# Choosing the experts of an image for six and two blocks of tokens in place of four, two and two

## The chip, the cores and the metric

The kernel runs on one core of one Trainium2 chip. Five engines work side by side, each through its own queue of instructions in order: TensorE (PE in the profile, with its weight loads as PEld), VectorE (DVE), ScalarE (ACT), GpSimd (POOL) and SyncE (SP), which issues most DMAs. The metric is the time of one execution on the device in microseconds (us); a reported time is the median of the runs.

## The reference

The input x is 4 images of 384 channels and 32 by 32 pixels. Layer 0 normalises groups of channels, runs a selective scan over the 1024 pixels in four directions with 16 states per channel, merges the directions, normalises, applies gelu and adds x. Layer 1 takes the pixels as 1024 tokens of 384 values: causal attention with one head is added, and then a mixture of four experts, of which each token uses two. What the change touches is the choice of the two experts:

```python
scores = jnp.einsum('bsd,de->bse', x, gate_w) + gate_b
probs = jax.nn.softmax(scores, axis=-1)
topk_vals, topk_idx = jax.lax.top_k(probs, TOP_K)            # TOP_K = 2 of 4 experts
mask = jnp.sum(jax.nn.one_hot(topk_idx, NUM_EXPERTS, dtype=probs.dtype), axis=-2)
masked = probs * mask
masked = masked / (jnp.sum(masked, axis=-1, keepdims=True) + 1e-09)
h = jax.nn.gelu(jnp.einsum('bsd,edh->ebsh', x, w1) + b1[:, None, None, :], approximate=False)
y = jnp.einsum('ebsh,ehd->ebsd', h, w2) + b2[:, None, None, :]
out = jnp.einsum('bse,ebsd->bsd', masked, y)
```

## The kernel before

**Ticks.** The order of all engines' work is written out by a loop over ticks. There are 768 units of the scan, 192 for each image, and each tick of the first 768 issues one: on ScalarE the decay da (an exponential), on VectorE the product v (front, L697) and the scan h (middle, L703), on GpSimd the product of h of the tick before with the C rows (back, L720), which is ordered behind v of its tick and so runs beside the scan. In image 0 TensorE makes some of the v instead. Every fourth tick TensorE adds four h into y (row, L745).

**Work beside the scan.** Attention and experts of image b are worked out during the scan of image b+1; those of image 3 follow the last tick. They are generators that go_on advances at the end of each tick: those in the list side get a step each tick, those in waiting (attention and experts) a budget of TensorE time. `yield "wait", 1` means: go on next tick; `yield "pe", x` means that about x us of TensorE work were issued, and a side generator stops for the tick when more than 1.0 is used up. What a step issues on VectorE stands in VectorE's queue after the scan of that tick and before v of the next.

**Shared buffers.** slots are eight SBUF buffers of 128 by 1024 floats that everything shares. They are handed out in the order in which they were given back, one tick after that at the earliest. banks are four PSUM banks shared in the same way.

**The choice of experts.** The 1024 tokens of an image are eight blocks of 128. As attention finishes blocks, ready (L1273) is started for a group of blocks: GROUPS = ((0, 4), (4, 2), (6, 2)), as first block and number. For its n blocks it normalises the rows, transposes them, computes the gate scores on TensorE (L1318) and adds the bias (sc, L1328). Then, all on small tensors of VectorE:

- exponents (L1343) and, a tick later, probabilities (L1348): softmax over the four experts;
- choice (L1353): each expert's score is compared with the others in cmp (n x 4 x 4), giving sel, the two best, and cum, running counts per expert;
- two ticks later kept (L1375): mk, the probabilities of the two chosen, normalised again;
- one tick later, with counts over the partitions and over the groups before that TensorE sums into pp: at, the row that a token would take in each expert's list, and from it spot and places, the two rows that it takes (L1427 to L1442). The last group also makes table (L1496): which expert and which rows each of 11 turns of 256 rows works on, and how many rows of the turn are filled (held_rows);
- mk is transposed (pm, L1468) and copied to a slot (mt);
- scatter (L1448): one block per tick, two indirect DMAs of GpSimd write the block's rows to the lists of its two experts in DRAM (xs_d);
- in the tick of the last scatter the shares (L1480 to L1486): for each of the two choices, which expert's row it is, times mk, summed; one tick later mt is stored to gates_d.

When the last group is routed, experts (L1544) loads rows from xs_d and the experts' weights on SP's queue, and works through the turns. For image 3 (alone in the code) the exponents and shares stand elsewhere, and only there are held_rows read, to skip empty rows on TensorE.

## Time and profile before

| | us |
|---|---|
| median of three runs | 3735.69 |
| lowest, highest | 3728.15, 3737.49 |
| the profiled execution | 3733.57 |
| its span, first to last instruction | 3731.8 |
| busy: PE, DVE, ACT, POOL | 3003.4, 2967.0, 2058.5, 1976.4 |
| granted TensorE clock, mean | 0.860 of full speed |

By stages, the busy time of the engines in us (0 to 850 is about image 0's scan, then the scans of images 1 to 3 with the attention and experts of images 0 to 2 beside them, then attention and experts of image 3):

| stretch | PE | DVE | ACT | POOL | DMA share |
|---|---|---|---|---|---|
| 0 to 850 | 555.0 | 736.9 | 614.2 | 526.0 | 0.60 |
| 850 to 1650 | 657.6 | 740.5 | 461.5 | 478.7 | 0.69 |
| 1650 to 2450 | 679.2 | 746.2 | 452.0 | 478.0 | 0.66 |
| 2450 to 3200 | 639.1 | 688.5 | 398.1 | 463.1 | 0.64 |
| 3200 to 3732 | 472.6 | 54.9 | 132.6 | 30.6 | 0.45 |

A row of a stretch is read against its length: VectorE is busy for 746 of 800 us in the third.

The lines of groups on the page give, after the engine and the operation, what is written and read, shapes, count, busy time and mean duration in ns, and the idle time of the engine before them with what ended it. A line that tells one instruction in order of time gives its start and its duration in us.

The choices of experts of images 0, 1 and 2 lie at about 934 to 1013, 1813 to 1897 and 2635 to 2722 us.

### The profile page before, as it was taken

Reading aid. Unit: us, or ns where it says so; the run is one execution under the profiler, and the core shown is the slowest. Engines: PE = TensorE matmul, PEld = TensorE weight load, DVE = VectorE, ACT = ScalarE, POOL = GpSimd, SP = SyncE. Lnnn points to the kernel's source line nnn. Section 1 sums busy time; section 2 is a strip of 40 time slices with the busy share of each in tenths; the row PEclk is TensorE's granted clock in tenths of the full one; section 3 lists DMA queues with packets and bytes.
Section 4 is the critical chain, followed back from the end, with each engine's and each line's share of the span. In section 5 each row is a group of like instructions: output and inputs, shape, how many; then the busy total and the mean of one; then the engine's idle time right before and its main releaser. Section 6 shows DMA issues by size and latency. Waiting matters only on the chain.

```text
span 3731.8 us, 41382 instructions
## 1 busy us (share of the span) xinstructions
PE 3003.4 (80%) x13281; PEld 1796.7 (48%) x13281; DVE 2967.0 (80%) x2338; ACT 2058.5 (55%) x3269; POOL 1976.4 (53%) x931
## 2 busy tenths in 40 slices
PE   4766666778489999769669999769679999788998
PEld 1333333334256555334336656334346665466776
DVE  6899888989979999998999999999989999220000
ACT  5787887556466566355546665445446664342221
POOL 2777667645645555764556656765656666110001
PEclk7677767789689999879779999879689999889997
DMA  5667555444478878644558978563468886215655
GB/s 188 217 255 286 208 209 204 170 166 161 165 242 282 305 269 296 223 172 140 188 200 288 320 250 300 192 211 127 139 226 304 284 291 225 75 62 162 200 188 168
DMA packets 405200, 798.41 MB, mean 214 GB/s; under 512 B 47500, under 2 KB 278620, under 8 KB 404972
## 3 DMA queue, kind: packets, MB, share of 16 engines
q1 hardware_dynamic: 390572, 770.01, 59.5%
q0 software_dynamic: 8192, 25.17, 2.0%
q8 instruction: 118, 1.93, 0.2%
q10 hardware_dynamic: 6208, 0.39, 0.1%
q14 instruction: 110, 0.90, 0.1%
HBM read 680.44 MB, written 115.02 MB: 213 GB/s over the span
## 4 chain that ended last, share of the span: by engine, by line
DVE 44%; PE 33%; ACT 7%; DMA 7%; issue 5%; POOL 2%; SPq 1%; DVEq 0%; ACTq 0%; POOLq 0%
DVE h L703 24%; DVE v L697 14%; PE ph L1680 7%; PE py L1730 6%; PE y L745 3%; DMA du<-dts 2%; DMA w<-in_w 2%; ACT da L196 2%; PE pq L1121 2%; ACT st L196 2%; PE v_end L1730 2%; PE pv L1132 1%; POOL h L720 1%; PE pdt L537 1%; PE y_end L1730 1%
## 5 line engine op out<-in xcount | busy, mean ns | idle before, releaser
L720 POOL TENSOR_TENSOR h<-h,bc 128x1024 f32<-128x1024 f32 x768 | 1812.8, 2364 | 1218.5 <-DVE v L697 1076.4
L703 DVE TENSOR_TENSOR_SCAN h<-da,v 128x1024 f32<-128x1024 f32 x768 | 1749.9, 2283 | 78.7 <-PE v L1009 41.1
L196 ACT ACTIVATE da<-dt,a 128x1024 f32<-128x1024 f32 x768 | 883.2, 1160 | 770.0 <-DVE h L703 643.9
L697 DVE TENSOR_TENSOR v<-du,bc 128x1024 f32<-128x1024 f32 x665 | 858.1, 1290 | 117.6 <-PE y L745 50.4
L745 PE MATMUL y<-h,sel 128*32 128x512 f32 x3072 | 572.1, 708 | 197.4 <-POOL h L720 189.8
L1680 PE MATMUL ph<-turned,w 128*128 128x256 f32 (+1 forms) x2784 | 637.0, 385 | 47.2 <-DMA w<-in_w 42.4
L1680 PEld LDWEIGHTS ph<-turned,w 128*128 128x128 f32 x2784 | 526.2, 194 | 166.8 <-issue 49.9
L1730 PE MATMUL py<-w,ht 128*128 128x384 f32 x1704 | 577.8, 491 | 3.9 <-DMA w<-in_w 3.8
L1730 PEld LDWEIGHTS py<-w,ht 128*128 128x128 f32 x1704 | 319.6, 191 | 259.5 <-issue 38.3
L745 PEld LDWEIGHTS y<-h,sel 128*32 128x32 f32 x3072 | 104.5, 120 | 534.6 <-POOL h L720 308.3
L196 ACT ACTIVATE ht<-ph,b1t 128x256 f32<-128x256 f32 x470 | 197.0, 472 | 281.2 <-PE ph L1680 260.4
L1789 POOL DMA_INDIRECT g<-ysd,places x64 | 83.9, 1310 | 342.8 <-DMA ysd<-yt 327.0
L196 ACT ACTIVATE st<-turn,bt 128x128 f32<-128x128 f32 x832 | 243.5, 546 | 0.1
L1009 PE MATMUL v<-ident,st 128*128 128x128 f32 x824 | 155.0, 350 | 87.1 <-DVE h L703 79.6
L1009 PEld LDWEIGHTS v<-ident,st 128*128 128x128 f32 x824 | 125.8, 182 | 134.4 <-DVE h L703 69.4
L186 ACT ACT_TABLE_LOAD x120 | 154.0, 1283 | 12.3 <-issue 10.2
L537 PE MATMUL pdt<-xd,wdt 12*128 12x512 f32 x184 | 114.8, 753 | 32.4 <-ACT st L196 17.0
L1450 POOL DMA_INDIRECT xsd<-fx,places x32 | 36.5, 1141 | 132.9 <-issue 132.3
L1749 DVE COPY yt<-y_end 128x384 f32<-128x384 f32 x3 | 1.7, 558 | 130.6 <-ACT ht L196 62.9
L1222 PE MATMUL po<-vt,pt 128*128 128x384 f32 x234 | 90.9, 539 | 13.1 <-ACT pt L1112 13.1
L1151 PE MATMUL ss<-axn,qt 128*128 128x512 f32 (+3 forms) x240 | 90.3, 519 | 3.4 <-ACT yb L1232 1.6
L196 ACT ACTIVATE ht<-ht 128x3072 f32<-128x3072 f32 x33 | 91.3, 2766 | 0.4
(411 smaller groups left out, 2710.8 us busy)
## 6 DMA issues: line engine op xcount, KB each, us to landing
w<-in_w SPq DMA_DIRECT2D x528, 384.0 KB
bc<-rows SPq DMA_DIRECT2D x384, 512.0 KB
dt<-dts SPq DMA_DIRECT2D x192, 512.0 KB
du<-dts SPq DMA_DIRECT2D x192, 512.0 KB
dts<-dt SPq DMA_DIRECT2D x48, 512.0 KB
dts<-du SPq DMA_DIRECT2D x48, 512.0 KB
xg<-xsd SPq DMA_DIRECT2D x44, 384.0 KB
ysd<-yt SPq DMA_DIRECT2D x44, 384.0 KB
```

The lines of the kernel that those rows point to most:

```text
L186: nc.scalar.preload_act_table_set(kind)
L196: return nc.scalar.activation(dst, src, f, **more)
L537: nc.tensor.matmul(pss[i], wdt[r, m * P : (m + 1) * P], xd[r, bass.ts(h, 512)], start=True, stop=True,)
L697: return nc.vector.tensor_tensor(u["v"], spread["du4", n], spread["bc", n][:, 0, :], ALU.mult)
L703: nc.vector.tensor_tensor_scan(u["h"][:, ::step], u["da"][:, ::step], u["v"][:, ::step], 0.0, op0=ALU.mult, op1=ALU.add,)
L720: product = units[n]["product"] = nc.gpsimd.tensor_tensor(h, h, spread["bc", n][:, 1, :], ALU.mult)
L745: units[n]["row"] = nc.tensor.matmul(y, sel, h, start=first, stop=last, tile_position=(0, jj * DJ))
L1009: nc.tensor.transpose(u["v"][:, t * P : (t + 1) * P], st[:, t, u["j"] * P : (u["j"] + 1) * P], ident)
L1151: nc.tensor.matmul(ps[:, : e - o], qt[:, c, i * P : (i + 1) * P], xn[o // 512][:, c, : e - o], start=(c == 0), stop=(c == M - 1 and (alone ...
L1222: nc.tensor.matmul(po[:, :C], pts[i][:, j, :], vt[:, j, :], start=False, stop=(j == i))
L1680: nc.tensor.matmul(ps[:, i * BT : i * BT + n], t[:, c, i * P : (i + 1) * P], xt[:, c, :n], start=(c == 0), stop=(c == M - 1),)
L1730: nc.tensor.matmul(pss[i][:, :C], hts[j][:, 2 * c + f, i * P : (i + 1) * P], tiles["2", j, c][0][:, f, :], start=(c == 0 and f == 0), stop ...
```

## The change

For the first three images the normalising, the transposes and the scores stay in groups of four, two and two, but the scores of the first four and the next two go into one tensor sc, and what follows is done once for all six, in a new function chosen: from exponents to shares. The last two blocks stay a group of their own. Image 3 keeps its three groups. Beside this, in all images:

- both choices stand in one tensor two, so that spot comes from one maximum instead of a minimum and a maximum, and the shares from three instructions instead of six;
- cmp is no longer a buffer of its own but a slot (for image 3 a buffer of the scan's decays, which is over by then);
- mk is transposed and copied in parts of up to four blocks, so six blocks take two banks, two slots and two stores to gates_d, the second part one tick after the first;
- held_rows are worked out for image 3 only;
- the small tensors, base and fresh are made large enough for six blocks, and the image's totals move to another column of pp;
- experts waits until all groups of the image are routed.

```diff
-    base = const.tile([P, E, 4], F32, tag="base", name="base")
+    base = const.tile([P, E, 6], F32, tag="base", name="base")
     fresh = {}
-    for n in (2, 4):
+    for n in (2, 4, 6):
...
+        def group_rows(q0, n):
+
+            if q0 + n > 4 and b not in routes:
                 routes[b] = Route(b)
-            return routes[b].rows[:, q0 - 4 : q0 - 4 + n]
+            return [
+                fx0[:, q, :] if q < 4 else routes[b].rows[:, q - 4, :] for q in range(q0, q0 + n)
+            ]
...
+    WIDE = ((0, 6), (6, 2))
...
-        sc = small("sc", name, n, E)
+        groups = GROUPS if alone else WIDE
+        g = [i for i, (g0, gn) in enumerate(groups) if g0 <= q0 < g0 + gn][0]
+        g0, gn = groups[g]
+        if (b, g) not in raw:
+            raw[b, g] = small("sc", f"{b}_{g}", gn, E), []
+        sc, whole = raw[b, g]
         nc.vector.tensor_tensor(
-            sc, pg[:, : n * E].rearrange("p (q e) -> p q e", e=E),
+            sc[:, q0 - g0 : q0 - g0 + n], pg[:, : n * E].rearrange("p (q e) -> p q e", e=E),
             gb.unsqueeze(1).to_broadcast([P, n, E]), ALU.add,
         )
         banks.give(f"pgate_{name}")
-
+        whole.extend(rows)
+        if len(whole) < gn:
+            return
+        yield from chosen(b, g, sc, whole)
...
+    def chosen(b, h, sc, rows):
+
+        alone = b == B - 1
+        name = f"{b}_{h}"
+        groups = GROUPS if alone else WIDE
+        last = len(groups) - 1
+        q0, n = groups[h]
+        parts = [range(o, min(o + 4, n)) for o in range(0, n, 4)]
...
         def choice():
-            cmp = [
-                one.tile([P, 4, E, E], F32, tag=f"cmp{i}", name=f"cmp{i}_{name}")[:, :n]
-                for i in range(2)
-            ]
+            both = cmp_.rearrange("p (i f) -> p i f", i=2)[:, :, : n * E * E]
+            both = both.rearrange("p i (q a b) -> p i q a b", a=E, b=E)
+            cmp = [both[:, i] for i in range(2)]
...
+        if alone:
+            cmp_ = dap.tile([P, L], F32, tag="da", name=f"cmp_{name}")
+        else:
+            cmp_ = yield from slots.take(f"cmp_{name}", P, L)
         cum = choice()
+        if not alone:
+            slots.give(f"cmp_{name}")
...
-        if h == LAST:
-            for i in range(LAST + 1):
+        if h == last:
+            for i in range(last + 1):
                 nc.tensor.matmul(
-                    pp[:, 4 * E : 5 * E], ones, last_of(i, False),
-                    start=(i == 0), stop=(i == LAST),
+                    pp[:, 8 * E : 9 * E], ones, last_of(i, False),
+                    start=(i == 0), stop=(i == last),
...
         spot = small("spot", name, n, 2)
-        two = [small(f"two{i}", name, E, n) for i in range(2)]
+        two = sm.tile([P, 2, E, 6], F32, tag="two", name=f"two_{name}")[:, :, :, :n]
         far = float(2 * E * CAP)
-        nc.vector.scalar_tensor_tensor(two[0], sel, -far, at, ALU.mult, ALU.add)
-        nc.vector.tensor_tensor(two[1], sel, at, ALU.mult)
-        nc.vector.tensor_reduce(
-            spot[:, :, 0], two[0].rearrange("p e q -> p q e"), AX.X, ALU.min
-        )
-        nc.vector.tensor_reduce(
-            spot[:, :, 1], two[1].rearrange("p e q -> p q e"), AX.X, ALU.max
-        )
-        nc.vector.tensor_scalar_add(spot[:, :, 0], spot[:, :, 0], far)
+        nc.vector.scalar_tensor_tensor(two[:, 0], sel, far, at, ALU.mult, ALU.subtract)
+        nc.vector.tensor_tensor(two[:, 1], sel, at, ALU.mult)
+        nc.vector.tensor_reduce(spot, two.rearrange("p i e q -> p q i e"), AX.X, ALU.max)
+        nc.vector.tensor_scalar(spot[:, :, 0], spot[:, :, 0], -1.0, far, ALU.mult, ALU.add)
         nc.vector.tensor_copy(places[b][:, q0 : q0 + n, :], spot)
...
-        pm = yield from banks.take(f"pm_{name}")
-        for q in range(n):
-            nc.tensor.transpose(pm[:E, q * P : (q + 1) * P], mk[:, q, :], ident)
-        yield "pe", 0.12 * n
-        mt = yield from slots.take(f"mt_{name}", E, 512)
-        yield "wait", 1
-        nc.scalar.copy(mt[:, : n * P], pm[:E, : n * P])
-        banks.give(f"pm_{name}")
+        mts = []
+        for part in parts:
+            pm = yield from banks.take(f"pm_{name}_{part[0]}")
+            for q in part:
+                o = (q - part[0]) * P
+                nc.tensor.transpose(pm[:E, o : o + P], mk[:, q, :], ident)
+            yield "pe", 0.12 * len(part)
+            mt = yield from slots.take(f"mt_{name}_{part[0]}", E, 512)
+            mts.append(mt)
+            yield "wait", 1
+            nc.scalar.copy(mt[:, : len(part) * P], pm[:E, : len(part) * P])
+            banks.give(f"pm_{name}_{part[0]}")
...
-        for i in range(2):
-            same = two[i]
-            nc.vector.tensor_tensor(
-                same, at, spot[:, :, i].unsqueeze(1).to_broadcast([P, E, n]), ALU.is_equal
-            )
-            nc.vector.tensor_tensor(same, same, mk.rearrange("p q e -> p e q"), ALU.mult)
-            nc.vector.tensor_reduce(
-                shares[b][:, q0 : q0 + n, i], same.rearrange("p e q -> p q e"), AX.X, ALU.add
-            )
-        yield "wait", 1
-        nc.sync.dma_start(gates_d[b][:, q0 * P : (q0 + n) * P], mt[:, : n * P])
-        slots.give(f"mt_{name}")
+        nc.vector.tensor_tensor(
+            two, at.unsqueeze(1).to_broadcast([P, 2, E, n]),
+            spot.rearrange("p q i -> p i q").unsqueeze(2).to_broadcast([P, 2, E, n]), ALU.is_equal,
+        )
+        nc.vector.tensor_tensor(
+            two, two, mk.rearrange("p q e -> p e q").unsqueeze(1).to_broadcast([P, 2, E, n]),
+            ALU.mult,
+        )
+        nc.vector.tensor_reduce(
+            shares[b][:, q0 : q0 + n, :], two.rearrange("p i e q -> p q i e"), AX.X, ALU.add
+        )
+        yield "wait", 1
+        for part, mt in zip(parts, mts):
+            o = (q0 + part[0]) * P
+            nc.sync.dma_start(gates_d[b][:, o : o + len(part) * P], mt[:, : len(part) * P])
+            slots.give(f"mt_{name}_{part[0]}")
...
         tables[b] = sm.tile([1, 3, NBLK], I32, tag="tables", name=f"tables_{b}")
-        nc.vector.tensor_copy(tables[b], which)
+        kept = 3 if b == B - 1 else 2
+        if kept == 3:
+            held_rows = which[:, 2, :]
...
+            nc.vector.tensor_scalar(held_rows, held_rows, n[:, 0:1], 0.0, ALU.add, ALU.max)
+            nc.vector.tensor_scalar_min(held_rows, held_rows, float(BT))
+        nc.vector.tensor_copy(tables[b][:, :kept], which[:, :kept])
...
-        while (b, LAST) not in routed:
+        groups = GROUPS if alone else WIDE
+        while not all((b, h) in routed for h in range(len(groups))):
```

## The prediction

> **What bounds the kernel now.** I read the page first, then the table by stages, then the order of time of VectorE and of GpSimd around the choice of experts of image 2, then the same stretches of images 0 and 1 and the chain of waits in them.
>
> ```profile
> span 3731.8 us, 41382 instructions
> DVE  6899888989979999998999999999989999220000
> L720 POOL TENSOR_TENSOR h<-h,bc 128x1024 f32<-128x1024 f32 x768 | 1812.8, 2364 | 1218.5 <-DVE v L697 1076.4
> L703 DVE TENSOR_TENSOR_SCAN h<-da,v 128x1024 f32<-128x1024 f32 x768 | 1749.9, 2283 | 78.7 <-PE v L1009 41.1
> L697 DVE TENSOR_TENSOR v<-du,bc 128x1024 f32<-128x1024 f32 x665 | 858.1, 1290 | 117.6 <-PE y L745 50.4
> ```
>
> Until about 3170 us VectorE is full: each of 768 ticks is a product v (1.29 us) and a scan (2.28 us), some 3.58 us, with GpSimd's product of the tick before (2.36 us) beside the scan. Everything else that VectorE does stands between a scan and the next v and lengthens that tick. After 3200 us VectorE is nearly idle and TensorE carries the experts of image 3. So a VectorE instruction saved in images 0 to 2 counts in full where nothing else holds the tick, and one saved in image 3 counts only on its short chain.
>
> The second reading is GpSimd beside it, in the choice of image 2. Columns: start, duration, engine, line.
>
> ```profile
> 2662.00 2.35 POOL L720 TENSOR_TENSOR h<-h,bc 128x1024 f32<-128x1024 f32 x1 [0.56 <-PE place L1405]
> 2664.50 1.80 POOL L1450 DMA_INDIRECT xsd<-fx,places  x1 [0.16 <-issue]
> 2666.61 0.96 POOL L1450 DMA_INDIRECT xsd<-fx,places  x1 [0.30 <-issue]
> 2667.59 2.36 POOL L720 TENSOR_TENSOR h<-h,bc 128x1024 f32<-128x1024 f32 x1
> ...
> 2664.18 1.26 DVE L697 TENSOR_TENSOR v<-du,bc 128x1024 f32<-128x1024 f32 x1
> 2665.47 2.29 DVE L703 TENSOR_TENSOR_SCAN h<-da,v 128x1024 f32<-128x1024 f32 x1
> 2667.67 2.31 DVE L1376 SCALAR_TENSOR_TENSOR mk<-cnt,sc 128x8 f32<-128x8 f32 x1
> 2670.02 0.16 DVE L1377 TENSOR_REDUCE red<-mk 128x2 f32<-128x8 f32 x1
> ```
>
> A pair of scatters (L1450) pushes GpSimd's product back by more than a scan. The tiny mk then takes 2.31 us instead of the some 0.17 of its neighbours: it ends just after the product does (2669.95). So a tick after a pair of scatters is bound by GpSimd, and small work on VectorE under the scatters is partly free. In the pair above no small work preceded v at 2664.18, and the first scatter took 1.80 us, ending after v. The pair at 2659.13 and 2660.46, under the choice of blocks 4 and 5, took 1.03 and 0.97 and delayed nothing.
>
> [...] The trace: a cmp of 32 elements takes 0.19 us, of 64 elements 0.225. From those two I estimate 0.26 for 96.
>
> **The change, part by part.** An instruction that depends on the one before it starts 0.20 to 0.26 us after it, an independent one 0.10.
>
> *What is removed.* Counted in the code: from the exponents to the shares a group has 30 VectorE instructions before and 26 after (the minimum and maximum become one reduction; six share instructions become three). Three groups and a table of 21 made 111 per image; two groups and a table of 13 make 65. So 46 fewer for each of three images, 12 fewer for the last. By their starts in image 2: probabilities and choice 2.11 us for four blocks and 1.92 for two, which become one run of six; seven of its instructions grow by about 0.03, so 2.3. mk and its normalisation: 1.06 and 0.73 plus its blocked first, become 1.1. Places: 0.91 and 0.89 become 0.85. Shares: 1.0 and 0.8 become 0.62. Exponents: 0.34 saved. Table: from 2707.87 to 2709.50, 1.63 saved. The group of blocks 6 and 7: 0.1 at its places, 0.3 at its shares. In all 7.1 us per image.
>
> *What is moved.* Placing and scattering of blocks 0 to 3 now wait for blocks 4 and 5. Call T0 the tick in which the scores of the first four come (v at 2631.86 to v at 2635.83). The scores of 4 and 5 come in T4, those of 6 and 7 in T10. Before, scatters are issued in T5 to T8 (blocks 0 to 3), T9, T10, then T15, T16. After: choice of six in T5, mk in T7, places and first transposes in T8, the second transposes cost one more tick (T9), scatters of blocks 0 to 5 in T10 to T15, blocks 6 and 7 still in T15 and T16. T15 gets four scatters. The choice of 6 and 7 keeps its ticks, so the last scatter and the start of the experts stay in T16. SP's queue: the gates' DMA becomes two in T16, about 0.5 us each of issue with data long ready; xg behind them waits for the scatters anyway.
>
> *The ticks of image 2*, measured before, and after by these rules: v waits for the product; the product waits for the pair and the v before it; a scatter that meets v ends some 0.9 us after it. T0 −0.4; T1 −2.1 (choice of four gone); T3 −1.05 (its mk); T4 −0.85 (its places gone, exponents of six); T5 +0.4 (choice of six instead of two); T7 6.53 to 4.7, −1.8; T8 6.23 to 4.43, −1.8 (no scatters under either now); T10 7.06 to 5.25 (its shares and their blocking gone; eviction stays), −1.8. Then the scatters' new places. T11 0: pair under the scores, choice of 6 and 7 after it. T12 +0.1. T13 4.62 to 6.55, +1.9: pair bare under T12, mk waits. T14 8.01 to 7.1, −0.9: table shorter by 1.63, blocked 0.75. T15 +0.85: shares of six and a short wait. T16 6.59 to 7.65, +1.05: four scatters. T17 +0.2. Sum −6.2. As a check, 7.1 us of instructions less, stalls about the same: about 7.3 us before (T7 2.2, T8 0.9, T10 1.0, T11 0.3, T16 2.2, T17 0.7).
>
> *Other images.* Image 0 has the same order and no idle VectorE there: −6.2. In image 1, VectorE waits 3.94 us for TensorE (y L745) in T0, so T0's gain is lost, and I give back half of T1's: −4.9. Image 3 keeps three groups: its places are 0.1 us shorter in each, its shares 0.4 shorter after the scatter. I take −0.3; none or −0.8 are the ends.
>
> *Unknowns.* cmp now takes one of the eight shared slots and so waits for whoever last read that slot. Slots come back in order of release, and attention's were released several ticks before, so I take 0. The upper end is a transfer of 512 KB still under way, once per image: the longest in the chain of waits is 11.56 us (du<-dts at 2317.34). The reductions over four dimensions are costed as those over three: 0 to 0.1 us each. Could the gain be lost at the experts' start? There VectorE stalls 10.87 us in image 0 and 6.63 in image 2 on a row sum behind the first weights; that chain begins with the last scatter, which itself moves earlier, so I let it through. If it did not pass, half the gain could go.
>
> **Sum.** 6.2 + 4.9 + 6.2 + 0.3 = 17.6 us. The profiled execution took 3733.57: 3716.0. The median of the runs shown is 2.1 above it, so 3718.
>
> **Rivals.** (a) *Absorbed*: TensorE and the weights set the pace at the experts' start, or attention's end holds T1. For it: 18% of the chain is TensorE's outside the last 540 us (33% in all, the tail 14.5%). Against: in T0 to T17 of images 0 and 2 VectorE shows no wait for TensorE. Half the gain, −9: 3727. (b) *Slower: cmp waits for its slot.* Where the slot's last reader is a store of image preparation, VectorE stands between a scan and v, and GpSimd behind it, until that store lands: at 11.56 us in each of three images, 34.7 − 17.6 = +17, 3753. It decides from 5.9 us per image. For it: in image 1 two stores of 512 KB leave at 1829 and 1830, four ticks before the choice of six. Against it: the oldest released slot is taken, and in image 2 no store is near. (d) *Bare scatters.* The small work that covered them is gone. A bare pair makes 5.59 us from product to product (2662.00 to 2667.59), 2.0 more than a tick; seven such and 1 for the four in T15 are 15 per image instead of 7.3: +7.7 − 7.1, nothing gained, 3738. Against it: T10, T11, T13 and T14 do have work of blocks 6 and 7. (c) *More*: each removed instruction gives its full 0.2 us and stalls shrink: 46 × 0.2 × 3, 28 us, 3708. That the change does other than it says I exclude: blocks, places and scatters are all still there.
>
> **How the numbers follow.** Forecast 0.56, (a) 0.17, (b) 0.10, (c) 0.11, (d) 0.06. A measurement of this kernel tells about 0.3%, 11.2 us, from no change. Faster by more: the forecast nearly whole, (c), and a little of (a): 0.68. Within: most of (a), most of (d) and the forecast's edge: 0.21. Slower: (b) and the rest of (d), 0.11. Range 3706 to 3734: from (c) with 2 us of noise to past (a).
>
> **What would show it.** VectorE has 150 instructions fewer (2338 to 2188). T0 to T10 are about 9 us shorter, T11 to T17 about 3 longer. One mk of six blocks per image is short, and the mk of blocks 6 and 7 takes about 2.3 us where it took 0.3. Scatters stand bare in T12 and four of them in one tick. Wrong would be a cmp that waits for a slot, stalls of 14 us or more per image, or experts that start a tick or more later.

## The result and the profile after

The changed kernel takes 3706.61 us (median of 5 runs, 3705.43 to 3712.27) against 3735.69. The ratio is 0.9931, with a 95% interval of 0.9917 to 0.9946: 25.8 us less, between 20.2 and 31.0. The forecast was 17.6 us less, 3718; the median lies 0.6 us inside the lower end of the stated range (3706 to 3734). The profiled execution took 3705.43 us, of which the span is 3703.4.

The lines of the page that answer to those shown of before:

```profile
span 3703.4 us, 41159 instructions
DVE  6898888999979999998999999999999998220000
L720 POOL TENSOR_TENSOR h<-h,bc 128x1024 f32<-128x1024 f32 x768 | 1813.6, 2366 | 1189.3 <-DVE v L697 1033.9
L703 DVE TENSOR_TENSOR_SCAN h<-da,v 128x1024 f32<-128x1024 f32 x768 | 1749.5, 2283 | 78.4 <-PE v L1009 33.4
L697 DVE TENSOR_TENSOR v<-du,bc 128x1024 f32<-128x1024 f32 x665 | 871.2, 1310 | 105.7 <-PE y L745 46.6
```

The scan and the product are what they were; VectorE is as full. Its 2338 instructions are 2188, and GpSimd stands 29 us less idle before its products (1218.5 to 1189.3). Where did this time go from? Every tick has one scan, so the k-th scan of one execution can be set against the k-th of another: a difference that arises between scans 633 and 634 belongs to that tick. T0 is tick 240, 438 and 633 in images 0, 1 and 2. From the starts of the scans in the two traces, after minus before, in us:

| tick | forecast for image 2 | image 2 | image 0 | image 1 |
|---|---|---|---|---|
| T0 | -0.4 | -0.27 | 0.01 | -0.31 |
| T1 | -2.1 | -1.98 | -1.98 | -2.67 |
| T3 | -1.05 | -1.08 | -1.08 | -1.10 |
| T4 | -0.85 | -0.89 | -0.88 | -0.89 |
| T5 | +0.4 | 0.41 | 0.44 | 0.41 |
| T6 | 0 | 0 | -0.71 | 0 |
| T7 | -1.8 | -1.94 | -1.93 | -1.92 |
| T8 | -1.8 | -1.70 | -1.53 | -1.02 |
| T9, T10 | -1.8 | -1.77 | -3.03 | -3.11 |
| T11, T12 | +0.1 | 0.70 | 0.97 | 0.95 |
| T13 | +1.9 | 2.01 | 0.67 | 1.11 |
| T14 | -0.9 | -0.75 | -0.80 | -0.75 |
| T15 to T17 | +2.1 | 2.27 | 2.27 | 2.20 |
| sum | -6.2 | -4.99 | -7.58 | -7.10 |

The same differences, added over longer stretches and for every kernel of this study against the first profile of before. The choices are ticks 240 to 264, 432 to 456 and 632 to 656; the experts are ticks 264 to 360, 456 to 584 and 656 to 767; the rest is all else, with the end of image 3. The ratio is over the timed runs. The runs e5 to e8 were made on another chip and e12 on a third, each beside the kernel before on the same chip, so kernels are compared by their ratios; medians are compared for runs of one chip alone.

| kernel | choices | experts | rest | ratio, 95% interval |
|---|---|---|---|---|
| changed | -20.6 | -11.7 | +4.0 | 0.9931, 0.9917 to 0.9946 |
| e1 changed again | -20.3 | -9.7 | -0.3 | 0.9931, 0.9918 to 0.9944 |
| e2 three groups | -8.2 | -6.2 | +0.3 | 0.9962, 0.9948 to 0.9975 |
| e3 long table | -12.2 | 0.0 | +1.1 | 0.9963, 0.9950 to 0.9976 |
| e4 early scatters | -19.2 | -7.6 | +10.4 | 0.9940, 0.9928 to 0.9953 |
| e5 padded | +4.1 | -8.2 | +0.8 | 0.9999, 0.9990 to 1.0008 |
| e6 before, padded | +9.7 | -3.5 | -1.6 | 1.0031, 1.0019 to 1.0043 |
| e7 lean | -21.6 | -4.1 | -0.7 | 0.9936, 0.9920 to 0.9952 |
| e8 four and four | -31.7 | -1.1 | +11.6 | 0.9935, 0.9919 to 0.9950 |
| e9 early weights | -36.5 | -13.7 | +7.6 | 0.9898, 0.9882 to 0.9914 |
| e10 before, slot | +0.2 | -3.9 | -1.3 | 0.9998, 0.9987 to 1.0008 |
| e11 before again | -0.5 | -3.7 | -1.6 | one run only |
| e12 before, early weights | -17.2 | -4.9 | +10.5 | 0.9959, 0.9947 to 0.9970 |

The first two columns of the changed kernel are the result: 20.6 us in the choices, where 17.3 were forecast, and some 6 to 12 us in the experts' stages between them, where nothing was forecast. The second part is seen in single profiles only: of the timed 25.8 us the choices leave 5.2, and with the interval anything from 0 to 10. The rest lies mostly before the choice of image 0 and behind the last scan. The first of these differs by 4.2 us between the two executions of the kernel before, the second by 5.4 us between the two of the changed kernel, so I read nothing from it.

How a pair of scatters, now bare, pushes the product back is seen in GpSimd's order of time in image 2 of the changed kernel (start, duration, engine, line):

```profile
2658.37 1.01 POOL L1474 DMA_INDIRECT xsd<-fx,places  x1 [0.17 <-issue]
2659.69 1.98 POOL L1474 DMA_INDIRECT xsd<-fx,places  x1 [0.31 <-issue]
2661.69 2.36 POOL L720 TENSOR_TENSOR h<-h,bc 128x1024 f32<-128x1024 f32 x1
2664.21 1.81 POOL L1474 DMA_INDIRECT xsd<-fx,places  x1 [0.17 <-issue]
2666.33 0.96 POOL L1474 DMA_INDIRECT xsd<-fx,places  x1 [0.31 <-issue]
2667.30 2.36 POOL L720 TENSOR_TENSOR h<-h,bc 128x1024 f32<-128x1024 f32 x1
...
2681.61 1.09 POOL L1474 DMA_INDIRECT xsd<-rows,places  x1 [0.15 <-issue]
2683.00 1.06 POOL L1474 DMA_INDIRECT xsd<-rows,places  x1 [0.30 <-issue]
2684.37 0.96 POOL L1474 DMA_INDIRECT xsd<-rows,places  x1 [0.30 <-issue]
2685.63 0.96 POOL L1474 DMA_INDIRECT xsd<-rows,places  x1 [0.30 <-issue]
2686.62 2.35 POOL L720 TENSOR_TENSOR h<-h,bc 128x1024 f32<-128x1024 f32 x1
```

From product to product 5.61 us pass (2661.69 to 2667.30), as the prediction had it for a bare pair (5.59). The four scatters of T15 are there, from 2681.61. VectorE in the same image:

```profile
2630.26 0.18 DVE L1374 TENSOR_TENSOR sc<-sc,red 128x24 f32<-128x24 f32 x1
2630.47 0.26 DVE L1382 TENSOR_TENSOR cmp<-sc 128x96 f32<-128x96 f32 x1
...
2639.24 0.32 DVE L1399 SCALAR_TENSOR_TENSOR mk<-cnt,sc 128x24 f32<-128x24 f32 x1
...
2667.39 2.31 DVE L1399 SCALAR_TENSOR_TENSOR mk<-cnt,sc 128x8 f32<-128x8 f32 x1
```

The comparison starts 0.21 us after the instruction that it depends on: no wait for its slot. The mk of six blocks is short (0.32), and that of blocks 6 and 7, which took 0.29 before, now takes 2.31 beside the product at 2667.30. In images 0 and 1 it takes 1.04 and 1.25.

### The profile page after: what moved, and what is told of

The parts are those of the page before. It is cut to its first block, busy times and chain, and to the rows that moved or that the text cites. A ratio compares the mean times of both kernels' runs of the same rounds, so it can differ in the third digit from the quotient of the medians.

```text
span 3703.4 us, 41159 instructions
## 1 busy us (share of the span) xinstructions
PE 2985.5 (81%) x13251; PEld 1787.3 (48%) x13251; DVE 2948.8 (80%) x2188; ACT 2058.9 (56%) x3266; POOL 1973.0 (53%) x933
## 3 DMA queue, kind: packets, MB, share of 16 engines
q8 instruction: 118, 1.93, 0.2%
## 4 chain that ended last, share of the span: by engine, by line
PE 30%; DVE 29%; DMA 3%; issue 2%; ACT 2%; SPq 1%; POOL 1%; DVEq 0%; POOLq 0%; ACTq 0%
DVE h L703 16%; DVE v L697 10%; PE ph L1714 8%; PE py L1764 7%; PE y L745 2%; DMA w<-in_w 2%; PE v_end L1764 2%; PE y_end L1764 1%; PE pq L1121 1%; PE pv L1132 1%; DMA du<-dts 1%; PE y_end L1714 1%; PE v_end L1714 1%; ACT ht L196 1%; POOL h L720 1%
## 5 line engine op out<-in xcount | busy, mean ns | idle before, releaser
L720 POOL TENSOR_TENSOR h<-h,bc 128x1024 f32<-128x1024 f32 x768 | 1813.6, 2366 | 1189.3 <-DVE v L697 1033.9
L697 DVE TENSOR_TENSOR v<-du,bc 128x1024 f32<-128x1024 f32 x665 | 871.2, 1310 | 105.7 <-PE y L745 46.6
L745 PE MATMUL y<-h,sel 128*32 128x512 f32 x3072 | 564.6, 701 | 208.5 <-POOL h L720 201.5
L186 ACT ACT_TABLE_LOAD x120 | 154.0, 1283 | 12.1 <-issue 10.0
L537 PE MATMUL pdt<-xd,wdt 12*128 12x512 f32 x184 | 112.6, 745 | 36.6 <-ACT st L196 20.3
```

The source lines that it names most:

```text
L186: nc.scalar.preload_act_table_set(kind)
L537: nc.tensor.matmul(pss[i], wdt[r, m * P : (m + 1) * P], xd[r, bass.ts(h, 512)], start=True, stop=True,)
L697: return nc.vector.tensor_tensor(u["v"], spread["du4", n], spread["bc", n][:, 0, :], ALU.mult)
L720: product = units[n]["product"] = nc.gpsimd.tensor_tensor(h, h, spread["bc", n][:, 1, :], ALU.mult)
L745: units[n]["row"] = nc.tensor.matmul(y, sel, h, start=first, stop=last, tile_position=(0, jj * DJ))
```

## The experiments

Each edit is against the changed kernel, or against the kernel before where it says so.

**e1, the changed kernel again**

> The changed kernel, unchanged, a second time. The trace of the changed kernel showed 20.6 us gained in the ticks of the three choices (7.9, 6.8, 5.9) and 11.6 us more between them, in the experts of images 0, 1 and 2 (5.5, 4.6, 1.5), less 3.75 us lost after the last scan. Theory L (the extra belongs to this kernel's order of transfers and ticks): the same three numbers again within 1 us each, time 3705 to 3709 us. Theory R (the extra is how transfers fell in that one execution): the choices again 20 to 21 us, but the experts' 11.6 us differ by 3 us or more, and the time goes with them.

Measured 3705.69 us (3703.52 to 3710.43). The choices repeat to 0.3 us in sum: 7.6, 8.4 and 4.3 against 7.9, 6.8 and 5.9, and every tick from T1 to T17 to 0.02. What differs are a few ticks around them that wait for TensorE (tick 438 by 1.6 us, tick 654 by 1.6). The experts give 5.7, 2.5 and 1.5 in place of 5.5, 4.6 and 1.5; the stretch after the last scan is 1.6 us shorter than before where it was 3.75 longer. So the gain in image 0's experts belongs to the kernel; of image 1's, half moved between two executions; and the loss at the end did not come again. Neither theory holds whole.

**e2, three groups again**

```diff
-    WIDE = ((0, 6), (6, 2))
+    WIDE = GROUPS
```

> Keeps the shorter table and the fused places and shares, and chooses in groups of four, two and two again. Predicted terms: of the 7.1 us of VectorE work per image the table is 1.63 and the fused shares and places about 1.3 (1.0 + 0.8 + 0.8 of shares become about 1.5, places 0.2 less), so merging is about 4.2 per image, 12 us in all. Theory M (merging pays, stalls equal): 8 to 13 us slower than the changed kernel, 3715 to 3720. Rival S (the new scatter places cost more than the merged choice saves): within 4 us of the changed kernel or faster. Where the experts' ticks lie differently, the extra gain of 11.6 us should change by more than 3 us if it comes from the places of the ticks, and stay if it comes from the parts that both share.

3719.24 us, ratio 0.9962: 11.6 us slower than the changed kernel (0.31% of 3735). Its choices give 8.2 us, 12.1 to 12.5 less than with six and two. The merging was forecast at 4.2 per image: theory M. The experts give 6.2, of it 3.4 in image 0, so three groups have a part of that gain too.

**e3, the long table**

```diff
-        kept = 3 if b == B - 1 else 2
+        kept = 3
```

> The changed kernel with the eight instructions of the table's third row worked out for images 0 to 2 too. Theory M (the table stands between scan and product in full): 1.63 us for each of three images, 4.9 us slower, 3711 to 3712. Rival C (a pair of scatters stands over that tick, and the table is covered): less than 1.5 us slower in all.

3718.99 us, 12 to 13 us slower than the changed kernel. The table itself is 1.51, 1.53 and 1.51 us (tick T14 in each image), 4.6 in all, as theory M has it and against C. What the other 7 to 9 us are is not shown. In the trace tick T0 waits 1.2 and 1.3 us longer for TensorE in images 0 and 1 (for attention's output, and for the row sums y), and the experts give 0.0 in place of 10 to 12. But T0 of image 0 comes before anything that this edit adds, and of the experts' loss the largest parts stand in ticks 460 and 530, which move by 2.6 and 1.8 us between the two executions of the changed kernel.

**e4, scatters one tick earlier**

```diff
+        todo = [] if alone else list(range(n))
+        if todo:
+            yield "wait", 1
         mts = []
         for part in parts:
+            if todo:
+                scatter(todo.pop(0))
...
-            for q in range(n):
-                scatter(q)
-                if q < n - 1:
+            while todo:
+                scatter(todo.pop(0))
+                if todo:
                     yield "wait", 1
```

> The changed kernel with the scatters of blocks 0 to 5 begun one tick earlier, beside the transposes of mk, which they don't need. No tick has four scatters then. In the trace of the changed kernel ticks T15, T16, T17 of image 2 are 0.7, 0.3 and 1.3 us longer than before. Theory B (the burst of four costs this): 1.5 to 2.3 us less per image, 5 to 7 us faster than the changed kernel, about 3700. Rival N (a pair costs about 2 us wherever it stands, bare or after another pair): the time stays within 2 us. Should the first pair meet a product v, 0.9 us per image comes back.

3711.93 us, not faster: 5 to 6 us slower by the medians, where rival N had said within 2. In image 2 the burst is gone and T15 to T17 are 2.7 us shorter than in the changed kernel, but T10, T11 and T14, under which the pairs now stand, are 0.8, 1.3 and 0.9 longer: 2.9 given back. In images 0 and 1 the same ticks give back 3.8. This is rival N by the ticks: moving the pairs changes where they cost and gains nothing.

**e5, the changed kernel padded**

```diff
             nc.vector.tensor_tensor(cmp[0], cmp[0], cmp[1], ALU.max)
+            for _ in range(26 if h == 0 and not alone else 0):
+                nc.vector.tensor_tensor(cmp[0], cmp[0], cmp[1], ALU.max)
```

> The changed kernel with 26 VectorE maxima of 96 elements, which change nothing, put into the choice of six of images 0 to 2 (tick T5), 0.25 us each as dependent ones: 6.5 us per image, so the choices last about as long as before the change. The extra gain in the experts of images 0 to 2 was 11.7 and 9.7 us in two executions of the changed kernel, 6.2 with three groups, 7.6 with the early scatters and 0.0 with the long table. Theory A (the experts' gain or loss is how VectorE's ticks fall against TensorE's chain, which any VectorE work in the choice shifts): the experts' gain is another number, differing by 3 us or more from 10, and the total is 19.5 us of padding plus or minus that. Theory O (the gain comes with what the changed kernel emits: stores of the gates later in SP's queue, slots taken for the comparisons): the experts' gain stays at 9 to 12, and the time is 3725 to 3727.

3732.19 us. The padding took more than I had put: in VectorE's order of time

```profile
2647.83 7.57 DVE L1389 TENSOR_TENSOR cmp<-cmp 128x96 f32<-128x96 f32 x26
```

26 in 7.57 us, 0.29 each, and T5 grew by 7.6 us in every image, 22.8 in all. By the ratios the padded kernel is 25.4 us slower than the changed one (19 to 32). The experts give 8.2, with choices that are even longer than before: nearer to theory O, and against A as I had put it, though the time is above O's. No other tick from T1 to T17 moved by more than 0.02 us, so T5 pays for VectorE's work in full.

**e6, the kernel before padded**

```diff
             nc.vector.tensor_tensor(cmp[0], cmp[0], cmp[1], ALU.max)
+            for _ in range(16 if h == 1 and not alone else 0):
+                nc.vector.tensor_tensor(cmp[0], cmp[0], cmp[1], ALU.max)
```

> The kernel before with 16 VectorE maxima of 32 elements, which change nothing, put into the choice of blocks 4 and 5 of images 0 to 2: 0.2 us each, 3.2 us per image. Theory A (where the ticks fall): the experts of images 0 to 2 gain or lose 3 us or more against the kernel before, most likely a gain, since all five kernels tried beside it had none or a gain; total 9.6 us of padding less that, so 3734 to 3744. Theory O (what is emitted): the experts stay within 2 us, and the time is 3743 to 3745.

3744.52 us, at the seam of the two theories: T5 is 3.6 us longer per image, 10.8 in all, and the ratio says 11.6 (7.1 to 16.1). The experts give 3.5 in sum, as much as a second execution of before gives (e11). Inconclusive by the time, but not by the ticks: 342 and 346 are 1.4 and 0.4 us shorter although nothing but padding was added.

**e7, the lean choice**

```diff
             exponents()
             yield "wait", 1
-            probabilities()
...
-            nc.vector.tensor_scalar_add(red, red, 1e-9)
             nc.vector.reciprocal(red, red)
```

> The changed kernel without the normalisation of the probabilities (three VectorE instructions per group) and without the small constant added to the sum of the two kept (one), since the kept two are normalised anyway and their sum is at least the largest exponential, 1. Eight instructions less per image 0 to 2, twelve less in image 3. Theory F (each removed small instruction on the full VectorE gives its 0.2 us): 1.6 us per image in the choices, 4.8 us, and up to 1 us in the last image's chain: 3700 to 3702. Rival H (the instructions of blocks 6 and 7 lie under scatters and give nothing): half of it, 3703 to 3705. The experts' part may shift by some us either way and is read apart.

3707.45 us, ratio 0.9936: no gain. By the ticks, T5 is 0.42 to 0.49 us shorter than in the changed kernel, T7 and T13 0.2 each and T11 0.1, some 1.0 us per image where 1.6 were expected; the three instructions of blocks 6 and 7 in T11 gave 0.12 us instead of 0.6. That is rival H by the ticks. Its 3 us do not show in the time; in this trace the experts gave 4.1 in place of 9.7.

**e8, four and four**

```diff
-    WIDE = ((0, 6), (6, 2))
+    WIDE = ((0, 4), (4, 4))
...
-            cum = sm.tile([P, (24, 8, 8)[h]], F32, tag=f"cum{h}", name=f"cum_{name}")
+            cum = sm.tile([P, (24, 16, 8)[h]], F32, tag=f"cum{h}", name=f"cum_{name}")
```

> The changed kernel with groups of four and four in place of six and two: as few VectorE instructions, the scatters of blocks 0 to 3 in T5 to T8 as before, those of blocks 4 to 7 in T15 to T18. The experts of images 0 to 2 begin two ticks, some 8 us, later. Theory E (TensorE is busy for 96 percent of the experts' stages, so a later start is paid): the experts' stages lose 4 to 8 us per image, time 3715 to 3730. Rival P (VectorE's ticks pay for nothing but their own work there): within 4 us of the changed kernel.

3708.36 us, the same as six and two within the interval: rival P by the time. By the parts neither theory describes it. Of the 31.7 us of the choices 10.8 are tick 262 of image 0, 14.4 us long before: with the experts starting later, no row sum waits behind them there. The experts of images 1 and 2 give back 8.9 and 4.6, as theory E has it, and those of image 0 gain 14.5. Since all this work stands two ticks later, a tick no longer holds the same work in both traces, and of the 11.6 us of the rest 6.3 lie before the first choice.

**e9, the first weights earlier**

```diff
         while not all((b, h) in routed for h in range(len(groups))):
+            if b in tables and fetched[0] < 4 and slots.ready(1 + slots.kept):
+                weights()
             yield "wait", 1
```

> The changed kernel with the first four weight chunks of images 0 to 2 asked for one per tick from the tick of the table on, as far as slots are free, and not all together behind the gathered rows. In the changed kernel VectorE waits 10.6 us at 1046.5 (image 0, third tick before the experts' stage) for the row sums y, which stand in TensorE's queue behind the first expert's ph, and ph waits for weights that were asked for at 1025.6 to 1030.7. Theory W (the late weights make that wait): it shrinks by 5 us or more in image 0 and by 2 to 4 in images 1 and 2; 8 to 15 us faster than the changed kernel, 3692 to 3699. Rival D (TensorE's work for the first expert itself, at a clock of 0.5, stands before y whenever the weights come, or the chunks take DMA time from the rows that the ticks need): less than 3 us, 3704 to 3707.

3694.0 us, ratio 0.9898 (0.9882 to 0.9914): the fastest of all, theory W. Only two of the four chunks of image 0 found a free slot early: they were asked for at 992.97 and 997.02 us, in place of 1025.57. TensorE of the changed kernel in order of time, at the start of image 0's experts:

```profile
1019.36 1.51 PE L1652 MATMUL pxg<-ident,xg 128*128 128x128 f32 x6 [4.40 <-DMA xg<-xsd]
1031.17 8.05 PE L1714 MATMUL ph<-turned,w 128*128 128x256 f32 x24 [10.30 <-DMA w<-in_w]
1039.06 2.74 PE L463 MATMUL pxd<-x,wx 128*128 128x512 f32 x6
1041.64 2.75 PE L1714 MATMUL ph<-turned,w 128*128 128x256 f32 x12
1044.32 1.92 PE L745 MATMUL y<-h,sel 128*32 128x512 f32 x16
```

and VectorE beside it:

```profile
1033.65 2.29 DVE L703 TENSOR_TENSOR_SCAN h<-da,v 128x1024 f32<-128x1024 f32 x1
1046.52 1.23 DVE L697 TENSOR_TENSOR v<-du,bc 128x1024 f32<-128x1024 f32 x1 [10.59 <-PE y L745]
```

The rows xg are there at 1019, the weights only at 1031; ph stands at the head of TensorE's queue, y behind it, and v waits 10.59 us for y. TensorE in e9:

```profile
1021.92 1.51 PE L1652 MATMUL pxg<-ident,xg 128*128 128x128 f32 x6 [4.50 <-DMA xg<-xsd]
1023.68 6.29 PE L1714 MATMUL ph<-turned,w 128*128 128x256 f32 x24 [0.25 <-ACT turned L1658]
1029.81 2.74 PE L463 MATMUL pxd<-x,wx 128*128 128x512 f32 x6
1033.76 2.83 PE L1714 MATMUL ph<-turned,w 128*128 128x256 f32 x12 [1.22 <-DMA w<-in_w]
1036.52 1.92 PE L745 MATMUL y<-h,sel 128*32 128x512 f32 x16
```

ph follows pxg at once, and the v behind y waits 0.3 us for GpSimd instead. Tick 262 falls by 10.3 us against the changed kernel and tick 654 by 5.6; image 1 gains nothing there.

**e10, the kernel before with its comparisons in a slot**

```diff
-            cmp = [
-                one.tile([P, 4, E, E], F32, tag=f"cmp{i}", name=f"cmp{i}_{name}")[:, :n]
-                for i in range(2)
-            ]
+            both = cmp_.rearrange("p (i f) -> p i f", i=2)[:, :, : n * E * E]
+            both = both.rearrange("p i (q a b) -> p i q a b", a=E, b=E)
+            cmp = [both[:, i] for i in range(2)]
...
+        if alone:
+            cmp_ = dap.tile([P, L], F32, tag="da", name=f"cmp_{name}")
+        else:
+            cmp_ = yield from slots.take(f"cmp_{name}", P, L)
         cum = choice()
+        if not alone:
+            slots.give(f"cmp_{name}")
```

> The kernel before with one part of the change alone: the comparisons of images 0 to 2 in one of the shared slots, as a pair in one tensor. Measured against the sum of the ticks of the choices, kernels with three groups and with six and two, which share this part, had 3 to 7 us less than those ticks explain. Theory O (the slots' rotation moves the experts' transfers): 3727 to 3731, the experts' stages 3 us or more shorter than in the kernel before. Theory A (nothing but where ticks fall): the ticks of the choices are those of before, so the time is that of before within 2 us. Rival (b) of the prediction: a wait for the slot, up to 11.6 us in each image, slower.

3729.83 against 3731.18 us, ratio 0.9998 (0.9987 to 1.0008): no difference. The slot is neither a wait, which settles rival (b) of the prediction, nor the cause of the experts' gain. The experts' 3.9 us are as many as the 3.7 of e11, but not the same: 2.0 of them are in image 0 (ticks 342 and 346), where e11 has 0.1.

**e11, the kernel before again**

> The kernel before, a second profiled execution. All seven other kernels show the ticks 336, 342 and 346 (experts of image 0) shorter by 0.8, 1.4 and 0.4 us than the first execution of before, also the one that only pads it. If these 2.6 us were that execution's own, the second shows them shorter too. The waits of 2.8 us at tick 351 and of 2.2 us at tick 559 for the rows bc: there again if they belong to the kernel before, gone if they were that execution's own.

3727.75 us in its one run. Its experts are 3.7 us shorter than in the first execution, all of it in image 1 (tick 530, 1.7). Ticks 342, 346 and 351 are as long as before (within 0.03, 0.00 and 0.4 us), so these three came again; tick 336 is shorter by 0.5, tick 559 by 0.7. Read against this profile, the experts' gain of the changed kernel is 8.0 and 6.0 us in its two executions, not 11.7 and 9.7.

**e12, the kernel before with the early weights**

```diff
         while (b, LAST) not in routed:
+            if b in tables and fetched[0] < 4 and slots.ready(1 + slots.kept):
+                weights()
             yield "wait", 1
```

> The kernel before with the early weight chunks of e9 alone, and nothing of the change. In e9 the wait for y at the experts' start fell by 10.3 us in image 0, by 0 in image 1 and by 5.6 us in image 2 against the changed kernel, 15.9 us of ticks, and the median by 12.6. Theory W: the same waits are there in the kernel before (14.43 and 10.19 us ticks), so this alone brings 10 to 16 us: 3717 to 3722. And the change on top of it then measures as e9 against this kernel: if only the ticks of the choices are its gain, 20 to 21 us (3694 against 3714 to 3716); if the experts' part belongs to it too, 25 to 28 us (3694 against 3719 to 3722).

3724.93 against 3738.6 us on that chip, ratio 0.9959: 15.3 us less, theory W. The ratio of e9 to e12, 0.9898 / 0.9959 = 0.9939, makes the change 22.8 us on top of the early weights; with both intervals it is 15 to 30, so it does not tell 21 from 26.

## Where the experts' gain comes from

Only image 0's part repeats. It is 5.5 and 5.7 us in the two executions of the changed kernel, 3.5 to 5.7 in the other kernels with six and two, 3.4 with three groups (e2), 2.7 and 2.0 in e6 and e10, and 0.1 and 0.0 in e11 and e12. Image 1's part goes from 5.8 us of gain to 4.2 of loss over the kernels that keep these ticks, and the two executions of the kernel before alone differ by 3.7 in it.

Image 0 can be followed in the traces. TensorE in the kernel before, in order of time, just ahead of tick 342:

```profile
1369.82 4.91 PE L1680 MATMUL ph<-turned,w 128*128 128x256 f32 x22
1375.64 2.83 PE L1680 MATMUL ph<-turned,w 128*128 128x256 f32 x12 [0.91 <-ACT ht L196]
1380.20 0.85 PE L1618 MATMUL pxg<-ident,xg 128*128 128x128 f32 x6 [1.73 <-DMA xg<-xsd]
1381.33 7.11 PE L1680 MATMUL ph<-turned,w 128*128 128x256 f32 x24 [0.28 <-DMA w<-in_w]
1388.37 1.92 PE L745 MATMUL y<-h,sel 128*32 128x512 f32 x16
```

The granted clock in the same stretch, as a table of windows (after the stretch and its length, the busy time of TensorE; the last three columns are clock, DMA share, GB/s). The windows are 3.41 us long because all changes of the granted clock in the traces of before and of the changed kernel fall on steps of 3.413 us, each to within 0.01 us:

```profile
1374.76:1378.17 3.41, 2.52 (x12) 2.20 (x12) 3.38 (x2) 1.87 (x3) 2.15 (x2) 1.00 1.03 399
1378.17:1381.58 3.41, 1.40 (x9) 0.92 (x8) 3.34 (x3) 2.59 (x5) 2.15 (x2) 1.00 1.09 352
1381.58:1385.00 3.42, 3.42 (x9) 2.71 (x9) 3.35 (x3) 0.15 (x1) 2.10 (x2) 0.50 0.79 295
```

The changed kernel at the same place:

```profile
1361.76 7.50 PE L1714 MATMUL ph<-turned,w 128*128 128x256 f32 x34
1369.10 0.82 PE L1652 MATMUL pxg<-ident,xg 128*128 128x128 f32 x6
1369.97 5.42 PE L1714 MATMUL ph<-turned,w 128*128 128x256 f32 x24
1375.32 1.92 PE L745 MATMUL y<-h,sel 128*32 128x512 f32 x16
```

and e10:

```profile
1376.31 2.83 PE L1685 MATMUL ph<-turned,w 128*128 128x256 f32 x12 [0.20 <-DMA w<-in_w]
1380.89 0.85 PE L1623 MATMUL pxg<-ident,xg 128*128 128x128 f32 x6 [1.75 <-DMA xg<-xsd]
1382.02 5.42 PE L1685 MATMUL ph<-turned,w 128*128 128x256 f32 x24 [0.28 <-DMA w<-in_w]
1387.37 1.92 PE L745 MATMUL y<-h,sel 128*32 128x512 f32 x16
```

with its steps of the clock:

```profile
1376.48:1379.89 3.41, 2.65 (x12) 1.99 (x11) 3.34 (x3) 2.25 (x5) 2.37 (x1) 1.00 1.04 388
1379.89:1383.31 3.42, 2.14 (x12) 1.83 (x13) 3.35 (x3) 2.02 (x4) 2.36 (x1) 1.00 1.09 354
1383.31:1386.72 3.41, 3.41 (x18) 3.00 (x17) 3.34 (x3) 1.84 (x3) 2.36 (x1) 1.00 1.00 330
```

Before, TensorE pauses 0.91 us and then 1.73 us, the clock falls to 0.50 for one step, the next 24 ph take 7.11 us instead of 5.42, and the row sums y come that much late: v of tick 342 waits 1.46 us. In e10 and e6 the first pause is 0.2 to 0.3 us, the second the same 1.75; the clock stays at 1.00, and tick 342 is 1.4 us shorter. The second pause is as long there as before, but it lies across two steps: TensorE is busy for 0.78 and 0.63 of them in e10, where before it was busy for 0.41 of one (1.40 of 3.41 us). In the changed kernel there is no pause. Its y after these ph starts 13.05 us earlier than before (1375.32 against 1388.37), while VectorE's tick 351 starts 10.0 us earlier. SP asks for the rows bc behind a store that waits for TensorE's chain, at 1407.23 in place of 1420.36 us; they come in time, and tick 351, 2.8 us of waiting before, is a plain one. Tick 342 is short in every kernel but before, e11 and e12; tick 351 is 2.3 to 2.7 us shorter in the seven executions with six and two, 0.9 in e2, and at most 0.4 in the rest, four and four among them.

The pauses are for weights and for xg, both issued by SP (the first one of before ends by its trace with ht, that of e6, e10, e11 and e12 with weights). Before, the waits of SP's queue from 1336 to 1374 us begin with

```profile
SPq L1585 <- DMA dts<-dt: 5.7, 1, 5.7
```

(total us, times, longest): a weight chunk, which takes a shared slot that the store of dt still reads, is held until that store lands, and all of SP's queue with it. After, the same wait is 3.2 us:

```profile
SPq L1619 <- DMA dts<-dt: 3.2, 1, 3.2
```

In the other traces it is 5.3 to 6.0 us in e2, e6, e10, e11 and e12, and 2.9 to 4.2 in all seven executions with six and two. So it goes with tick 351, which waits 1.9 to 2.9 us for bc in the first and at most 0.5 in the others; it does not go with tick 342, which is short in e2, e6 and e10 too. That store belongs to VectorE's ticks, the chunk behind it to TensorE's chain, so I take the wait to be decided by how the two run against each other; no run tests this alone. Which instruction of the change sets this offset is not settled: a slot (e10) and a shorter choice (e5 keeps the gain with a longer one) are excluded, and three groups (e2) keep a third of tick 351's part.

## Why the prediction was right, and where it was short

*VectorE full, and each saved instruction counts between scan and v*: right. The ticks carry it, and e5 shows it from the other side: 22.8 us of padding, 25.4 us by the ratios.

*The removed instructions*: 150, as counted. Merging 4.2 per image, measured 4.1 (e2); table 1.63, measured 1.51 (e3); a comparison of 96 elements put at 0.26 us, measured 0.26. The reductions over four dimensions took no more than those over three: 0.18 us for 16 elements in both (spot of blocks 6 and 7 after, shares of four blocks before).

*Pairs of scatters moved under bare ticks*: right in kind and nearly in size. T11 to T17, without T14, lose 5.0 us in image 2 where 4.1 were forecast, and 3.9 and 4.3 in images 0 and 1.

*v waits for the product, the product for the pair and the v before it, and a scatter that meets v ends some 0.9 us after it*: right in the new places. In image 2 of the changed kernel the six scatters that start while a v runs end 0.83 to 0.88 us after it and take 1.06 to 1.98 us; the other ten take 0.96 to 1.09. Six of the seven products behind a pair or the four start within 0.03 us of the last scatter's end, the seventh (2679.12) waits 1.77 us for v. The mk of blocks 6 and 7 ends 0.03 to 0.04 us after the product beside it in each of the three images, and so takes 2.31 us in image 2. A v that starts beside a product is held too. Before, in image 2:

```profile
2721.84 2.35 POOL L720 TENSOR_TENSOR h<-h,bc 128x1024 f32<-128x1024 f32 x1
2723.35 1.94 DVE L697 TENSOR_TENSOR v<-du,bc 128x1024 f32<-128x1024 f32 x1
```

This v takes 1.94 us and ends 1.10 us after the product; after, the v at 2663.19 takes 1.96 us and ends 1.10 us after its product (2661.69). The scan is not held: 750 of the 768 scans of before lie beside a product in part or whole, and none takes more than 2.29 us.

*Image 2 taken for images 0 and 1*: mis-sized. T9 and T10 give 3.03 and 3.11 where 1.8 was put, T13 loses 0.67 and 1.11 where 1.9 was put, since mk of blocks 6 and 7 takes 1.04 and 1.25 us there and not 2.31. In image 1 I gave back half of T1's gain to a wait for TensorE; it came whole and more, 2.67. Together T0 to T17 give 19.7 and the choices with the few ticks around them 20.6, where 17.3 were forecast. That the sum is so near is in part luck: image 2, worked out tick by tick, gave 5.0 in place of 6.2, and images 0 and 1 gave 7.6 and 7.1 in place of 6.2 and 4.9.

*Image 3, 0.3 us*: not to be told. The stretch after the last scan was 3.75 us longer in one execution of the changed kernel and 1.6 us shorter in the other.

*"I let it through" at the experts' start*: the step that failed. The gain did pass, and rival (a) fell; but I took the experts' stages as a fixed length behind the choices. They depend on how SP's queue, TensorE's chain and VectorE's ticks run against each other, and there the profiles show another 6 to 12 us, of which 5.5 and 5.7 in image 0 came again. What in the change brings them stays open.

*The rivals*: (b) no wait for a slot in any trace, e10; (d) bare pairs cost what it said, but not 15 us an image. (c) named 3708, close to the time, and for a wrong reason: 138 instructions gave 20.6 us in the choices, 0.15 each and not 0.20, and the bare ticks grew. e7 shows why: of eight more instructions per image three were under scatters and gave 0.12 us in all.

## What to carry to other kernels

Where one engine is full tick after tick, set the k-th tick of one trace against the k-th of the other: sums of waits hide what this shows term by term, and a second execution of both kernels tells which terms are an execution's own. Price a saved instruction only in ticks that nothing else holds, and measure the cost of moved work at its new place. Before a wait is blamed on the engine named, look at what stands ahead in that engine's queue: here two chunks of weights asked for some 30 us earlier at the start of image 0's experts took 10.3 us from one wait, and early weights in all were worth 12 to 15 us, half as much as the change itself.

## What the runs showed of the hardware

In the traces of before and of the changed kernel the granted TensorE clock changed only on steps of 3.413 us. In before, e11 and e12 a pause of 1.73 to 1.75 us and the short one behind it (0.28 to 0.29 us) fell into one such step, in which TensorE was busy for 0.41 of the time, and the next step had a clock of 0.50. In e6, e10 and e2 pauses of 1.75, 1.75 and 1.63 us lay across two steps, with TensorE busy for 0.74 and 0.66, 0.78 and 0.63, and 0.75 and 0.72 of them, and the clock stayed at 1.00. In before and the changed kernel, from the first record of the clock on (26 us after the start), each of the 148 steps at full clock with TensorE busy for less than 0.40 was followed by half the clock, and so were 43 of the other 1407. The clock fell with no single pause over 1.75 us in before, e11 and e12, and in the changed kernel it stayed at 1.00 in the step after a pause of 3.02 us (to 219.24 us), which lay across two steps busy for 0.49 and 0.44. So where a pause falls counts beside its length.

A store that one engine's results feed held the weights of another for 5.7 us before and 3.2 us after, where the weights take the buffer that the store reads. And a small dependent VectorE instruction of 96 elements repeated every 0.29 us (e5), where its own duration is 0.26.
